# The last two attention heads in two halves of the queries, with the first group's output projection, norms, router and scatter between their tiles

## The chip, the cores and the metric

The kernel runs on one core of one Trainium2 chip. The metric is the device time of one launch in microseconds (us). The engines are named as in the profile: PE (TensorE, matmuls), PEld (its weight loads), DVE (VectorE), ACT (ScalarE), POOL (GpSimd), SP (SyncE, which here issues DMAs). ACT and POOL issue DMAs too.

## What is computed

One transformer layer in fp32, on 2048 tokens of 256 features. The attention has 16 heads of 128, unmasked, its four weight matrices as 4-bit codes with a scale per 32 rows. The second part is a mixture of 8 experts (hidden size 176), of which each token uses its best two.

```python
x = x + layernorm(attention(layernorm(x)))
x = x + layernorm(experts(layernorm(x)))
# attention
q, k, v = x @ wq + bq, x @ wk + bk, x @ wv + bv          # 2048 x (16 heads x 128)
out = softmax(q @ k.T / sqrt(128)) @ v                    # per head, 2048 x 2048 scores
return out @ wo + bo                                      # 2048 x 2048 times 2048 x 256
# experts
w, idx = top_k(softmax(x @ Wr), 2); w = w / sum(w)
h = silu(x @ Wg[e]) * (x @ Wu[e]);  y[e] = h @ Wd[e]
return sum over the token's two experts of w * y[e]
```

## The kernel before

**Order.** There is no planner: each engine runs its instructions in the order in which the code emits them, and waits by semaphore for its operands. So the place of a call in the code is its place in the queue of every engine it uses. Many tiles (`ph`, `pl`, `kT`, `v`, `oi`, `xr`, `xT0`, `xq`, `yg`, raw weights) come from one ring of 21 buffers with the tag `x` (`NX = 21`).

**The loop.** `for g in range(NS + 2)` (L851, `NS` = 256) takes one tile of 128 queries of one head per turn; head = g // 16, tile t = g % 16. The two extra turns drain the pipeline. A turn issues

- the scores of the tile against the 2048 keys in two halves (`scores_half`: 8 matmuls L525, L526, L529, and DVE's row max L530 each), the negated row max on DVE (`negmax`, L534), and two exponentials with row sums on ACT (`softmax`, L541);
- for the tile before: the reciprocal of the sums (L548, L551), the fp16 high part of the probabilities on ACT (`high_part`, L555) and, in two halves, the low part on DVE (`low_half`, L570). Each part goes through a DMA transpose issued by SP (L558, L576) into `pth` and `ptl`, which hold four tiles, a block, and come from one pool `pt` of two buffers each;
- two units of `pv_unit` (6 matmuls each, L597), which multiply the transposed probabilities of a finished block with V, 13 units behind (`PVLAG`); a block has 8. Its result is split into fp16 parts and written to `ot_d` in DRAM, but for head 15, which stays on chip (`o_last`);
- `fill(h, t)`: a part of the projections of Q, K or V of the next heads on PE (`proj_qk`, L240; `proj_v`), copied by ACT and split by POOL.

In heads 14 and 15 the loop has more: `early(t)` in head 14 makes the output bias row `crow` and issues the first loads of `oi` (attention output of four heads, read back from `ot_d`, L709); `late(t)` in head 15 loads more of them and the gate/up weights of the first half (`load_gu`, L690), splits those into two parts (`split_gu`, L681 on ACT and L683 on POOL), and runs part of the output projection.

**The output projection** `op_mm(b, half, js)` multiplies for one block b of 512 tokens (four blocks; half = 256 tokens) the head groups j in js: 16 matmuls per j (L748). With the last of j = 0 to 2 ACT moves the sum out (L764) and POOL adds `crow` (L765); with j = 3 DVE adds the rest into `at` (L759) and takes statistics (L773, L775).

**After the loop** (L902 on). For each block: first layer norm and residual (`ln_a`: a power on POOL, L81; `ln_b1`: scaling L779 and add L791 on DVE; `ln_b2`: statistics and a power; `ln_c`: scaling), transposes of the normalised rows on PE, copied by ACT and split by DVE (`tr`, L963 to L965), fp16 row pairs `xr` (`rows`, L947 on ACT, L948 on DVE), router logits and best two (`route`, 24 matmuls L976, then DVE). Blocks 0 and 1 make group 0, blocks 2 and 3 group 1. For each group `place(g)` gives every pair of token and expert a row, sorted by expert and padded to 128 rows, `scatter(b)` writes the rows to `xs_d` in DRAM with eight indirect DMAs per block (POOL, L1053), and `load_xt` reads them back transposed (SP, L1074). Then come 12 units of two 128-row tiles per group, one step each: `widen` (DVE, L1088), `gate_up` (12 matmuls L1101), `turn` (4 transposes L1120), `down` (12 matmuls L1136, ACT copy to `ysb`, L1142, DMA to `ys_d`, L1143). `gather(b)` fetches the two result rows per token (POOL, L1159), and `mix`, `scale_y` and `finish` weigh, normalise and add them (DVE L1176, ACT L1194) and write the output. The table `HOOK` says after which step other work is issued: `tr`, `route` and norms of blocks 2 and 3 at steps 1 to 7, `place(1)` and their scatter at 8, the gathers, mixes and finishes of blocks 0 and 1 from step 16 on, those of blocks 2 and 3 after the last. The tiles of the units (`xw`, `sg`, `h`, `ht`, `ysb`) come from the pool `tl` with two or three buffers each.

In before, block 0's first layer norm starts at the loop's last turn, blocks 0 and 1 are routed after the loop, and `place(0)` with the first scatter follows them and the projection of block 2.

Of the kernel before, what the change touches and what calls it, by code (L numbers as in the profile page):

```python
# [11 lines left out]
HP = mybir.dt.float16  # L12
# [26 lines left out]
def sandwich(  # L39
# [164 lines left out]
    soft_ctx, pt_ctx = ExitStack(), ExitStack()  # L204
# [20 lines left out]
    def kq_tile(which, h, b):  # L225
        if which == "q":
            return kqv.tile([128, 2, 512], HP, name="qT", bufs=3)
        if b % 2 == 0:
            KP[h] = kqv.tile([128, 2, 2, 512], HP, name="kT", tag="x", bufs=NX)
        return KP[h][:, b % 2]  # L230
# [282 lines left out]
    pt = pt_ctx.enter_context(tc.tile_pool(name="pt", bufs=2, reuse_waits="tile"))  # L513
# [3 lines left out]
    PT, PTL = {}, {}  # L517

# [34 lines left out]
    def high_part(h, t, m, p):  # L553
        ph = kqv.tile([128, S], HP, name="ph", tag="x", bufs=NX)
        nc.scalar.activation(ph, p, AF.Copy, scale=m[:, 6:7])  # L555
        if t % 4 == 0:
            PT[(h, t // 4)] = pt.tile([128, 4, 16, 128], HP, name="pth")
        nc.sync.dma_start_transpose(  # L558
            out=PT[(h, t // 4)][:, t % 4], in_=ph
        )  # L560
        return ph
# [3 lines left out]
    def low_half(half, h, t, m, p, ph):  # L565
# [7 lines left out]
        if half == 1:  # L573
            if t % 4 == 0:
                PTL[(h, t // 4)] = pt.tile([128, 4, 16, 128], HP, name="ptl")
            nc.sync.dma_start_transpose(  # L576
                out=PTL[(h, t // 4)][:, t % 4], in_=LOW.pop((h, t))
            )
# [10 lines left out]
    def pv_part(h, b, e):  # L589
# [11 lines left out]
        if e == 7:  # L601
# [5 lines left out]
            if (h, b) == (NH - 1, 3):  # L607
# [21 lines left out]
    LASTQ = {0: 1, 1: 2, 4: 3}  # L629

    def fill(h, t):
        p = h // 2
        if h == 0 and t < 5:
            proj_v(0, 6 + 2 * t, 2, "pv", wide=soft)
        if h == NH - 1:
            if t in LASTQ:
                proj_qk("q", h, LASTQ[t], wide=soft)
        elif t in QK:
            kind, dh, b = QK[t]
            if h + dh < NH:  # L640
                proj_qk(kind, h + dh, b, wide=soft)
# [8 lines left out]
    def pv_unit(u):  # L650
        n, e = divmod(u - PVLAG, 8)
        if 0 <= n < 4 * NH:
            pv_part(n // 4, n % 4, e)
# [63 lines left out]
    NS = NH * NT  # L717
# [13 lines left out]
    def op_mm(b, half, js, tag="pj", part=3):  # L731
        if js[0] == 0:
            if half == 0:
                AT[b] = kqv.tile([128, 4, D], F32, name="at", tag="x", bufs=NX)
# [63 lines left out]
    def ln_c(b):  # L798
# [4 lines left out]
    GW_LOAD = {0: 0, 2: 1, 6: 2, 8: 3}  # L803
    GW_SPLIT = {5: 0, 7: 1, 9: 2, 11: 3}
    EARLY = {8: (0, 0, 0), 10: (0, 0, 1), 12: (0, 0, 2), 14: (0, 1, 0)}
    OI_LOAD = {
        1: (0, 1, 1), 3: (0, 1, 2), 9: (1, 0, 0), 10: (0, 0, 3), 11: (1, 0, 1), 12: (0, 1, 3),
        13: (1, 0, 2), 14: (1, 0, 3),
    }
    OI_USE = {  # L810
        2: (0, (0,)), 3: (0, (1, 2)), 5: (1, (0,)), 6: (1, (1,)), 7: (1, (2,)),
        13: (0, (3,)), 14: (1, (3,)),
    }

    def early(t):
# [11 lines left out]
        if t in EARLY:  # L827
            load_oi(*EARLY[t], eng=nc.scalar)

    def late(t):  # L830
        if t == 5:
            proj_ctx.close()
            rp = ctx.enter_context(tc.tile_pool(name="gw", bufs=1, side="right"))
            guw[0] = rp.tile([128, 2, E, 2 * I], F32R, name="gu0")
        if t in OI_USE:
            op_mm(0, *OI_USE[t], "pj", 2)
        if t in GW_SPLIT:
            split_gu(guw[0], GW_SPLIT[t], gst.pop(GW_SPLIT[t]), True)
        if t in GW_LOAD:
            i = GW_LOAD[t]  # L840
            gst[i] = load_gu(0, i, nc.scalar)
        if t in OI_LOAD:
            load_oi(*OI_LOAD[t], eng=nc.scalar)
        if t == 7:
            X1[0] = kqv.tile([128, 4, D], F32, name="x1_0", tag="x", bufs=NX)
            nc.scalar.dma_start(out=X1[0], in_=XV[:, 0])


    defer = False
    prev2 = None  # L850
    for g in range(NS + 2):  # L851
        h, t = divmod(g, NT)
        live = g < NS
        if live:
            m = small.tile([128, 8], F32, name="m", bufs=6)
            s0 = scores_half(h, t, 0, m)
            if g == 0:
                proj_v(0, 0, 2)
                proj_v(0, 2, 2, "pv")
                proj_v(0, 4, 2, "s", wide=soft)  # L860
        if prev is not None:
            recip(prev[2])
        if prev2 is not None:
            low_half(1, *prev2)
        flush()
        if defer:
            pv_unit(2 * g - 1)
            defer = False
        pv_unit(2 * g)
        if prev is not None:  # L870
            prev = (*prev, high_part(*prev))
        if live:
            s1 = scores_half(h, t, 1, m)
            negmax(m)
            p = softmax((s0, s1), m)
        if prev is not None:
            low_half(0, *prev)
        prev2 = prev
        first = live and (2 * g + 1 - PVLAG) % 8 == 0
        if not first:  # L880
            pv_unit(2 * g + 1)
        if live:
            fill(h, t)
        if first and h == NH - 1:
            defer = True
        elif first:
            pv_unit(2 * g + 1)
        if live:
            prev = (h, t, m, p)
        else:  # L890
            prev = None
        if live:
            weight_steps(h, t)
        if h == 0 and t in (8, 9, 10):
            tail_consts(t - 8)
        if 7 <= g < 15:
            dequant_wo(g - 7)
        if h == NH - 2:
            early(t)
        if h == NH - 1:  # L900
            late(t)
        if g == NS - 1:  # L902
            ln_a(0)
            for j in range(4):
                load_oi(1, 1, j, eng=nc.scalar)
            op_mm(1, 0, (0, 1, 2))
        if g == NS:
            ln_b1(0)
            op_mm(1, 0, (3,))
        if g == NS + 1:  # L910
            ln_b2(0)
            ln_c(0)
            op_mm(1, 1, (0, 1, 2))
            for j in range(4):
                load_oi(2, 0, j)
    UEND = 2 * (NS + 2)

    pv_unit(UEND)
    op_mm(1, 1, (3,))
    soft_ctx.close()  # L920
    grp = ctx.enter_context(tc.tile_pool(name="grp", bufs=1, side="right", reuse_waits="tile"))
    sel_m, hot, gap, cmb, pos, eid = [], [], [], [], [], []

    before_e = grp.tile([128, E, E], F32)
    starts = grp.tile([1, NTL], F32)

    def open_groups(pool):
        nc.gpsimd.iota(starts, [[128, NTL]], base=0, channel_multiplier=0,
                       allow_small_or_imprecise_dtypes=True)
        nc.vector.tensor_tensor(  # L930
            before_e, iota8.unsqueeze(1).to_broadcast([128, E, E]),
            iota8.unsqueeze(2).to_broadcast([128, E, E]), ALU.is_lt,
        )
        for g in range(2):
            sel_m.append(pool.tile([128, GT + 1, E], BF, name=f"sel_m{g}"))
            hot.append(pool.tile([128, 2, GT, E], BF, name=f"hot{g}"))
            gap.append(pool.tile([128, GT], F32, name=f"gap{g}"))
            cmb.append(pool.tile([128, 2, GT], F32, name=f"cmb{g}"))
            pos.append(pool.tile([128, 2, GT], U32, name=f"pos{g}"))
            eid.append(pool.tile([1, NTL], I32, name=f"eid{g}"))  # L940
# [4 lines left out]
    def rows(b, on_pool):  # L945
# [57 lines left out]
    def place(g, tag="pj"):  # L1003
        ps = aux_psum([128, GT + 1, E], F32, "rk", tag)
        nc.tensor.matmul(ps, before_m, sel_m[g], start=True, stop=False)
        for t in range(GT):
# [11 lines left out]
            lower, before_e, pad.unsqueeze(1).to_broadcast([128, E, E]), ALU.mult  # L1018
# [19 lines left out]
            starts.unsqueeze(2).to_broadcast([1, NTL, E]), ALU.is_le,  # L1038
# [45 lines left out]
    def widen(g, u):  # L1084
        n = len(tiles_of(u))
        xr = tl.tile([128, 4, 256], F32R, name="xw", bufs=3)
# [6 lines left out]
    def gate_up(g, u):  # L1093
# [12 lines left out]
        sg = tl.tile([128, 2, I], F32, name="sg", bufs=2)  # L1106
        h = tl.tile([128, 2, I], F32, name="h", bufs=2)
# [6 lines left out]
    def turn(g, u):  # L1114
# [6 lines left out]
        ht = tl.tile([IH, 2, 2, 2, 128], F32R, name="ht", bufs=2)  # L1121
# [6 lines left out]
    def down(g, u):  # L1128
# [12 lines left out]
        y = tl.tile([128, 2, D], F32, name="ysb", bufs=3)  # L1141
# [39 lines left out]
    def scale_y(b, half):  # L1181
        hs = slice(2 * half, 2 * half + 2)
        R3[(b, half)] = rstd_of(MV3[b][:, hs], 2, small)
        nb = small.tile([128, 2], F32, name="nb", bufs=2)
# [35 lines left out]

    nc.scalar.activation(sgv, ssc[:, 0:1], AF.Sigmoid)
    open_groups(grp)
    uwp = ctx.enter_context(tc.tile_pool(name="uw", bufs=1, side="right", reuse_waits="tile"))
    guw[1] = uwp.tile([128, 2, E, 2 * I], F32R, name="gu1")
    ln_a(1)
    load_x1(1)
    loads(2, 1)
    tr(0, 0, "s")
    tr(0, 1, "s")
    rows(0, True)  # L1230
    ust = [load_gu(1, i) for i in range(2)]
    ln_b1(1)
    for e in range(1, 3):
        pv_unit(UEND + e)
    op_mm(2, 0, (0, 1, 2), "s")
    ln_b2(1)
    route(0)
    for e in range(3, 5):
        pv_unit(UEND + e)
    op_mm(2, 0, (3,), "s")  # L1240
    ln_c(1)
    split_gu(guw[1], 0, ust[0], True)
    split_gu(guw[1], 1, ust[1], True)
    ust = [load_gu(1, i) for i in range(2, 4)]
    for e in range(5, 9):
        pv_unit(UEND + e)
    tr(1, 0, "s")
    tr(1, 1, "s")
    rows(1, True)
    route(1)  # L1250
    pt_ctx.close()
    tl = ctx.enter_context(tc.tile_pool(name="tl", bufs=1, reuse_waits="tile"))
    dw = tl.tile([IH, 2, E, 2, D], F32R)
    op_mm(2, 1, (0, 1, 2, 3), "s")
    place(0)
    scatter(0)
    scatter(1)
    load_x1(2)
    ln_a(2)
    loads(3, 0)  # L1260
    split_gu(guw[1], 2, ust[0], False)
    split_gu(guw[1], 3, ust[1], False)
# [97 lines left out]
```

## Time and profile before

| | us |
|---|---|
| three runs | 1834.75, 1836.46, 1836.72 (median 1836.46) |
| the profiled execution | 1836.82 |
| its span, first to last instruction | 1835.0 |
| loop, to the negated row max of the last tile (L534) | 1543.3 |
| from there to the end of the span | 291.7 |
| first matmul of the experts (L1101) | 1644.1 |
| first of the second group | 1721.7 |

The mean granted TensorE clock is 0.963 of full speed. The profile is of one execution. Rows of a timeline have the start, the length, engine, line and operation with its tiles, and in brackets the idle time before it and what ended it. Busy sums of DMA queues are shares of 16 engines; a stretch may show a share over 1, as packets of several queues overlap on an engine.

### The profile page before, as it was taken

How to read it: one execution, taken by the hardware profiler on the slowest of the kernel's cores; microseconds unless marked ns; L12 is line 12 of the kernel's file. 1: busy time of each engine (PE TensorE's matmuls, PEld its weight loads, DVE VectorE, ACT ScalarE, POOL GpSimd, SP SyncE). 2: the span in 40 equal slices, each digit the busy share in tenths (PEclk: the TensorE clock that was granted, in tenths of full speed). 3: DMA queues.
4: the chain of work that ended last, by engine and by line, in shares of the span. 5: the costliest groups of instructions: out<-in, count | busy, mean ns of one | idle time of the engine just before them, and what ended most of it. 6: DMA issues, size and time to landing. Idle time of an engine off the chain costs nothing. (4 is left out here: it accounts for less than half of the span.)

```text
span 1835.0 us, 25558 instructions
## 1 busy us (share of the span) xinstructions
PE 1700.0 (93%) x8536; PEld 881.6 (48%) x8536; DVE 1598.3 (87%) x2250; ACT 1363.2 (74%) x1747; POOL 978.1 (53%) x976
## 2 busy tenths in 40 slices
PE   7899999999999999999999999999999998949660
PEld 4344444444444444444444444444444454749660
DVE  6999999999999999999999999999999887557252
ACT  5888888888888888888888888888888875213141
POOL 5596566556655665556565656565454331161423
PEclk9899999999999999999999999999999999878785
DMA  9999999999999999999999999999999999861622
GB/s 292 186 195 207 196 202 198 206 198 201 200 197 202 199 199 195 207 197 193 206 200 198 197 202 206 195 202 201 191 189 205 222 226 228 237 180 51 157 95 80
DMA packets 1128477, 355.08 MB, mean 194 GB/s; under 512 B 1095244, under 2 KB 1112092, under 8 KB 1128348
## 3 DMA queue, kind: packets, MB, share of 16 engines
q1 hardware_dynamic: 1104300, 302.20, 90.1%
q0 software_dynamic: 12672, 35.17, 6.7%
q10 hardware_dynamic: 11376, 16.09, 2.8%
q8 instruction: 69, 1.13, 0.2%
q14 instruction: 60, 0.49, 0.1%
HBM read 44.83 MB, written 34.08 MB: 43 GB/s over the span
## 5 line engine op out<-in xcount | busy, mean ns | idle before, releaser
L541 ACT ACTIVATE p<-s,m,ssc 128x1024 f32<-128x1024 f32 x512 | 612.3, 1200 | 183.1 <-DVE m L534 169.4
L570 DVE SCALAR_TENSOR_TENSOR pl<-p,m,ph 128x1024 f16<-128x1024 f32 x512 | 733.1, 1432 | 6.6 <-ACT ph L555 5.9
L530 DVE TENSOR_REDUCE m<-s 128x1 f32<-128x1024 f32 x512 | 621.8, 1214 | 19.4 <-PE s L529 18.5
L555 ACT ACTIVATE ph<-p,m 128x2048 f16<-128x2048 f32 x256 | 513.0, 2004 | 55.2 <-ACT t L253 15.0
L597 PE MATMUL pv<-pth,v 128*128 128x512 f16 x2048 | 504.2, 379 | 1.1 <-DMA pth<-ph 0.9
L597 PEld LDWEIGHTS <-v 128*128 128x128 f16 x3072 | 300.5, 98 | 363.9 <-issue 4.1
L525 PE MATMUL s<-kT,qT 128*128 128x512 f16 x1024 | 388.9, 380 | 10.9 <-ACT p L541 10.0
L526 PE MATMUL s<-kT,qT 128*128 128x512 f16 x1024 | 389.0, 380 | 0.7 <-POOL kT L255 0.7
L529 PE MATMUL s<-kT,qT 128*128 128x512 f16 x1024 | 305.5, 380 | 0.0
L597 PE MATMUL pv<-ptl,v 128*128 128x512 f16 x1024 | 251.9, 379 | 0.0
L285 POOL CAST v<-t 128x256 f16<-128x256 f32 (+1 forms) x118 | 51.0, 432 | 279.3 <-ACT t L284 279.3
L254 POOL CAST qT<-t 128x512 f16<-128x512 f32 x63 | 77.8, 1235 | 222.8 <-ACT t L253 222.8
L286 POOL TENSOR_TENSOR v<-t,v 128x256 f16<-128x256 f32 (+1 forms) x118 | 177.3, 1502 | 9.6
L529 PEld LDWEIGHTS <-qT 128*128 128x128 f16 x1024 | 100.4, 98 | 122.3 <-issue 2.1
L526 PEld LDWEIGHTS <-qT 128*128 128x128 f16 x1024 | 100.2, 98 | 122.2 <-issue 17.6
L525 PEld LDWEIGHTS <-qT 128*128 128x128 f16 x1024 | 100.2, 98 | 108.5 <-issue 1.1
L541 ACT ACTIVATION_READ_ACCUMULATOR p<-s,m,ssc 128x1 f32 x512 | 99.1, 194 | 0.0
L617 POOL TENSOR_TENSOR o<-t,o 128x512 f16<-128x512 f32 x60 | 96.2, 1603 | 4.9
L255 POOL TENSOR_TENSOR kT<-t,kT 128x512 f16<-128x512 f32 x61 | 93.5, 1532 | 5.2
L1101 PE MATMUL s<-gu,xw 128*128 x276 | 58.0, 366 | 33.4 <-DVE xw L1088 31.6
L255 POOL TENSOR_TENSOR qT<-t,qT 128x512 f16<-128x512 f32 x63 | 85.6, 1359 | 5.1
L548 DVE TENSOR_SCALAR m<-m 128x1 f32<-128x1 f32 x256 | 53.9, 211 | 36.0 <-ACT p L541 24.5
(198 smaller groups left out, 1610.4 us busy)
## 6 DMA issues: line engine op xcount, KB each, us to landing
ot_d<-o POOLq DMA_DIRECT2D x60, 256.0 KB
oi<-ot_d ACTq DMA_DIRECT2D x12, 512.0 KB
oi<-ot_d SPq DMA_DIRECT2D x12, 512.0 KB
ys_d<-ysb ACTq DMA_DIRECT2D x22, 256.0 KB
xs_d<-zero SPq DMA_DIRECT2D x10, 512.0 KB
pth<-ph SPq DMA_TRANSPOSE x256
ptl<-pl SPq DMA_TRANSPOSE x256
xt<-in_L_attn_x SPq DMA_DIRECT2D x4, 512.0 KB
```

Source lines behind the costliest of these rows:

```text
L254: nc.gpsimd.tensor_copy(t[:, 0, :], t32)
L255: nc.gpsimd.tensor_tensor(t[:, 1, :], t32, t[:, 0, :], ALU.subtract)
L286: nc.gpsimd.tensor_tensor(v[:, 1, sl, :], t32, v[:, 0, sl, :], ALU.subtract)
L525: nc.tensor.matmul(s[:, j, :], q[:, 0, qc], k[:, 0, :], start=True, stop=False)
L526: nc.tensor.matmul(s[:, j, :], q[:, 0, qc], k[:, 1, :], start=False, stop=False)
L529: nc.tensor.matmul(s[:, j, :], q[:, 1, qc], k[:, 0, :], start=False, stop=True)
L530: nc.vector.tensor_reduce(m[:, half : half + 1], s, AX.XY, ALU.max)
L541: nc.scalar.activation(p[:, bass.ts(i, 1024)], s, AF.Exp, bias=m[:, 2:3], scale=ssc[:, 0:1], accum_out=m[:, 3 + i : 4 + i],)
L555: nc.scalar.activation(ph, p, AF.Copy, scale=m[:, 6:7])
L570: nc.vector.scalar_tensor_tensor(pl[:, cs], p[:, cs], m[:, 6:7], ph[:, cs], ALU.mult, ALU.subtract)
L597: nc.tensor.matmul(ps, V[(h // 2, c // 4)][:, i % 2, c % 4, dc], d[:, :, c, :], start=(n == 0), stop=(n == 47),)
L617: nc.gpsimd.tensor_tensor(o[:, :, 1, :], halves(t32), o[:, :, 0, :], ALU.subtract)
```

## The change

The loop's order changes in the last two heads (32 tiles, from turn `LATE` = 224). Write r = g - 224. Tiles 0 to 7 of head 14 run at r = 0 to 7, tiles 0 to 7 of head 15 at 8 to 15, then tiles 8 to 15 of head 14 at 16 to 23, and of head 15 at 24 to 31. With that the first half of all tokens (blocks 0 and 1) has all its heads finished half-way, and its further work is issued between the tiles of the second half:

- K and Q of head 15 and the rest of Q are projected at r = 0 to 9, one each (`LATE_QK`); head 13 projects the last V pair two token tiles at a time, and one Q part. The bias row moves from head 14 to head 12.
- `op_mm` of blocks 0 and 1 runs at r = 10 to 17 (j = 0 to 2: two j's on even r, one on odd) and 20, 21, 24, 25 (j = 3). Each `oi` is loaded by ACT one tile ahead (`OI_PLAN`).
- `CHAIN` puts the norms of blocks 0 and 1 at r = 22 to 28, `tr`, `rows` and `route` at r = 26 to 31.
- the two turns after the last tile issue `place(0)`, `op_mm` of block 2 (j = 0 to 2) and the first scatter.
- The gate/up weights of the first half are loaded and split after the loop, each second piece on POOL, the others on DVE; so are those of the second half and `dw` (from `draw`), whose loads now stand behind the transposed loads.
- In `HOOK`, `place(1)` and its scatter go from step 8 to step 6; both gathers of group 0 stand at step 16, its mixes at 21 and 22, its `scale_y` at 23 and 24, and its `finish` after the gathers of blocks 2 and 3.
- `pt` becomes two pools of one buffer each; `at` and the residual rows of blocks 0 to 2 get a pool `ex`; the units' `xw`, `ht`, `ysb` and a joint tile for `sg` and `h` come from the ring `x`.

```diff
+    NS = NH * NT
+    LATE = NS - 2 * NT
+    def place_of(g):
+        if g < LATE:
+            return divmod(g, NT)
+        half, r = divmod(g - LATE, NT)
+        return NH - 2 + r // 8, 8 * half + r % 8
...
+    LATE_QK = {
+        0: ("k", 15, 0), 1: ("k", 15, 1), 2: ("k", 15, 2), 3: ("k", 15, 3), 4: ("q", 15, 0),
+        5: ("q", 15, 1), 6: ("q", 14, 2), 7: ("q", 14, 3), 8: ("q", 15, 2), 9: ("q", 15, 3),
+    }
-    def fill(h, t):
+    def fill(g, h, t):
         p = h // 2
+        if g >= LATE:
+            if g - LATE in LATE_QK:
+                proj_qk(*LATE_QK[g - LATE], wide=soft)
+            return
...
+        elif h == NH - 3:
+            if t < 12:
+                proj_v(p + 1, 4 + t - 1, 2, wide=soft)
+            elif t == 13:
+                proj_qk("q", NH - 2, 1, wide=soft)
...
+    OP_PLAN = {
+        10: (0, 0, (0, 1)), 11: (0, 0, (2,)), 12: (0, 1, (0, 1)), 13: (0, 1, (2,)),
+        14: (1, 0, (0, 1)), 15: (1, 0, (2,)), 16: (1, 1, (0, 1)), 17: (1, 1, (2,)),
+        20: (0, 0, (3,)), 21: (0, 1, (3,)), 24: (1, 0, (3,)), 25: (1, 1, (3,)),
+    }
+    OI_PLAN = {}
+    for r, (b, half, js) in OP_PLAN.items():
+        for j in js:
+            OI_PLAN.setdefault(r - 1, []).append((b, half, j))
...
+    def late(r):
...
+        if r in OP_PLAN:
+            op_mm(*OP_PLAN[r], "pj", 2)
+        for i in OI_PLAN.get(r, ()):
+            load_oi(*i, eng=nc.scalar)
...
+        for f in CHAIN.get(r, ()):
+            f()
...
+    CHAIN = {
+        22: [lambda: ln_a(0), lambda: ln_b1(0)],
+        23: [lambda: ln_b2(0)],
+        24: [lambda: ln_c(0)],
+        26: [lambda: tr(0, 0), lambda: ln_a(1), lambda: ln_b1(1)],
+        27: [lambda: tr(0, 1), lambda: rows(0), lambda: ln_b2(1)],
+        28: [lambda: route(0), lambda: ln_c(1)],
+        29: [lambda: tr(1, 0)],
+        30: [lambda: tr(1, 1), lambda: rows(1)],
+        31: [lambda: route(1)],
+    }
...
-        h, t = divmod(g, NT)
         live = g < NS
+        h, t = place_of(g) if live else (NH, g - NS)
...
+        if g >= LATE:
+            late(g - LATE)
+        if g == NS - 2:
+            for j in range(3):
+                load_oi(2, 0, j, eng=nc.scalar)
+            X1[2] = ex.tile([128, 4, D], F32, name="x1_2")
+            nc.scalar.dma_start(out=X1[2], in_=XV[:, 2])
+        if g == NS - 1:
+            for j in range(3):
+                load_oi(2, 1, j, eng=nc.scalar)
+        if g == NS + 1:
+            for j in range(3):
+                load_oi(3, 0, j)
+            for half in range(2):
+                load_oi(2, half, 3)
+        if g == NS:
+            place(0)
+            op_mm(2, 0, (0, 1, 2), "pj", 2)
+        if g == NS + 1:
+            op_mm(2, 1, (0, 1, 2), "s", 2)
+            scatter(0)
+            scatter(1)
...
+    op_mm(3, 0, (0, 1, 2), "pj", 2)
...
+    op_mm(3, 1, (0, 1, 2), "s", 2)
+    for i in range(4):
+        split_gu(guw[0], i, gst.pop((0, i)), i % 2 == 1)
+    op_mm(2, 0, (3,), "pj", 2)
+    op_mm(2, 1, (3,), "s", 2)
+    ln_a(2)
...
+    for i in range(4):
+        gst[(1, i)] = load_gu(1, i)
...
+    ln_b1(2)
...
+    for i in range(4):
+        split_gu(guw[1], i, gst.pop((1, i)), i % 2 == 1)
+    ln_b2(2)
...
+    experts(0)
+    for q in range(6):
+        load_xt(0, q)
+    op_mm(3, 0, (3,), "pj", 2)
+    op_mm(3, 1, (3,), "s", 2)
+    ln_a(3)
+    ln_c(2)
+    draw = [load_d(q) for q in range(4)]
+    for q in range(2):
+        split_d(q, draw[q])
...
     HOOK = {
-        1: [lambda: tr(2, 0), lambda: ln_b1(3)],
...
-        8: [lambda: place(1), lambda: scatter(2), lambda: scatter(3)],
+        0: [lambda: tr(2, 0), lambda: tr(2, 1), lambda: rows(2)],
+        1: [lambda: ln_b1(3), lambda: split_d(2, draw[2]), lambda: split_d(3, draw[3])],
+        2: [lambda: ln_b2(3), lambda: route(2)],
+        3: [lambda: ln_c(3)],
+        4: [lambda: tr(3, 0), lambda: tr(3, 1), lambda: rows(3)],
+        5: [lambda: route(3)],
+        6: [lambda: place(1), lambda: scatter(2), lambda: scatter(3)],
...
+        NU + 4: [lambda: gather(0, range(4)), lambda: gather(1, range(4))],
+        NU + 9: [lambda: mix(0, range(4))],
+        NU + 10: [lambda: mix(1, range(4))],
+        NU + 11: [lambda: scale_y(0, 0), lambda: scale_y(0, 1)],
+        NU + 12: [lambda: scale_y(1, 0), lambda: scale_y(1, 1)],
```

## The prediction

> **What bounds the kernel now.** The first view is the page: busy time per engine and the 40 slices of 45.9 us.
>
> ```profile
> PE 1700.0 (93%) x8536; PEld 881.6 (48%) x8536; DVE 1598.3 (87%) x2250; ACT 1363.2 (74%) x1747; POOL 978.1 (53%) x976
> PE   7899999999999999999999999999999998949660
> DVE  6999999999999999999999999999999887557252
> PEclk9899999999999999999999999999999999878785
> ```
>
> The loop over 16 heads fills PE; the last seven slices do not. So there are two stages, and the change moves work from the second, slack one into the first, full one. The second view is the busy time by stretch (columns: stretch, length, then PE, PEld, DVE, ACT, POOL busy with counts, PE clock, DMA share, GB/s).
>
> ```profile
> 1200.00:1400.00 200.00, 199.50 (x956) 93.40 (x955) 192.33 (x239) 169.22 (x213) 106.01 (x104) 1.00 1.07 194
> 1620.00:1644.00 24.00, 0.00 (x0) 0.00 (x0) 12.48 (x26) 0.00 (x0) 16.25 (x15) 0.59 0.67 157
> 1691.00:1722.00 31.00, 13.00 (x84) 12.15 (x83) 7.09 (x15) 5.20 (x10) 15.54 (x16) 0.74 0.48 128
> 1740.00:1757.00 17.00, 5.42 (x35) 4.51 (x33) 1.74 (x3) 1.29 (x3) 10.70 (x12) 0.71 0.38 111
> 1792.00:1835.00 43.00, 0.00 (x0) 0.00 (x0) 10.96 (x36) 7.93 (x17) 18.10 (x20) 0.53 0.25 80
> ```
>
> In the loop PE has 0.5 us in 200 free, and DVE only 8: work put there is paid nearly in full. In the tail PE stands still for 24 us (first scatter), 18 of 31 (second scatter), 12 of 17, and the last 43. The chain of waits says what ends those gaps (start, us, what).
>
> ```profile
> 1544.37 14.37 DMA ptl<-pl
> ...
> 1609.73 1.11 POOL xs_d L1053
> ...
> 1629.27 0.96 POOL xs_d L1053
> ...
> 1644.11 3.87 PE s L1101 x12
> ...
> 1711.83 2.27 DMA xs_d<-xr,pos
> 1714.28 6.69 DMA xq<-xs_d
> ...
> 1740.01 7.49 another core or an unknown queue
> ```
>
> Sixteen row scatters take 1609.7 to 1630.2 (20.3 us with their gaps), their landing 2.3, the transposed load 6.7, and the experts' first matmul comes at 1644.1. The last line is a stall of the experts: ACT cannot write the next `ysb` (three buffers) while the rows of `ys_d` leave slowly beside the gathers.
>
> The third view, DVE's timeline, gives what a tile costs; the time between two L534 rows (the negated row max, one per tile) is a tile.
>
> ```profile
> 1516.29 0.27 DVE L534 TENSOR_SCALAR m<-m,ssc 128x1 f32<-128x1 f32 x1
> 1521.94 0.27 DVE L534 TENSOR_SCALAR m<-m,ssc 128x1 f32<-128x1 f32 x1
> 1527.59 0.27 DVE L534 TENSOR_SCALAR m<-m,ssc 128x1 f32<-128x1 f32 x1
> 1528.97 0.75 DVE L759 SCALAR_TENSOR_TENSOR at<-op,sig,at 128x512 f32<-128x512 f32 x1
> 1534.50 0.27 DVE L534 TENSOR_SCALAR m<-m,ssc 128x1 f32<-128x1 f32 x1
> ```
>
> A tile with nothing beside it is 5.65 us (DVE sets it), one with an output evict and its statistics 6.9. In head 15 a tile with 16 projection matmuls went 1456.40 to 1463.57 (7.17), one with 32 to 1472.29 (8.72), and there DVE waited on PE.
>
> **The sum.** I split the execution at L534 of tile 224 (the first that the change reorders, 1350.7), and of tile 255 (1543.26): 192.6 us of loop, then 291.7 to the end of the 1835.0 span. The execution's own time is 1836.82, 1.8 more than its span and 0.4 above the median 1836.46.
>
> *Head 13* gets 12 V tile projections in place of 8 (0.43 us of PE each) and one Q projection (0.855): +2.6, since PE is full there.
>
> *r = 0 to 9* (tiles 224 to 233): each carries one K or Q projection, 4 matmuls, 0.855 us. The other 24 matmuls of 512 columns take 5.12, so PE sets 6.0: 60.0. The new order of heads by itself moves no work; each block still has its 8 PV units, and two one-buffer pools alternate as one of two buffers did.
>
> *r = 10 to 17*: four tiles with 32 and four with 16 projection matmuls: 4 x (8.72 + 7.17) = 63.6, by the rows above.
>
> *Loads of `oi`* for these tiles are now issued one tile ahead; before, two to four. The issue stands on ACT behind both exponentials, 3.5 us after L534 (1467.11 against 1463.57), the matmuls 0.2 us ahead of the next L534 (1472.08 against 1472.29). So the lead is the tile less 3.7: 2.3 us at r = 10, 3.4 at 12, 14, 16, 5.0 at 11, 13, 15, 17. No row shows how long a load takes in the loop. From below: 512 KB in that queue's packets (11376 packets, 16.09 MB, 2.8% of 16 engines: 1414 bytes, 72 ns), each alternating with a transpose packet of 24 ns, is 23 x 96 ns = 2.2 us, and the undisturbed `ys_d` write landed 1.7 after its issue: an estimate of 3.9 for one load and 6.1 for the second of a pair, which leaves waits of 2.0 + 3 x 1.0 = 5 us. From above: the `draw` loads issued at 1597.8 were used at 1605.2, 7.4 us: 5.1 + 3 x 4.0 + 4 x 2.4 = 27. I take 10, nearer to the first, whose packets are those of this loop; range 5 to 27.
>
> The Trainium skill, "DMA: Bandwidth & Descriptors", rules for kernel authors, says to issue a DMA early and wait for it late, which speaks against a lead of one tile. Its fit for one DMA (issued from GpSimd, not ACT: about 2.0 us and bytes / 436e3) makes 3.2 us of 512 KB, an estimate from that page, and by it alone these waits would be about 1 and the time some 9 us lower.
>
> *r = 18, 19*: 11.3. *r = 20 to 25*: four tiles with an evict (6.9 each, ACT's and DVE's share), and with the first group's ln_a/ln_b1 (four scalings 1.38, add 1.23, statistics 1.40 + 0.36) and ln_c (1.37) on DVE: 6.9 + 6.9 + 9.45 + 7.35 + 8.3 + 6.9 = 45.8.
>
> *r = 26 to 31*: transposes `tr`, router rows and routing. PE gets 4 x 0.44 + 2 x 2.6 = 7.0 more, which alone would fit under a DVE-set loop. But DVE's part of `tr` (0.68) needs ACT's copy of the same PSUM tile, and ACT issues that behind the tile's exponentials (2.9 us after L534), so DVE stands about 2.4 more per `tr`; rows cost 1.2 of DVE, a route 1.85. Sum 12.05 + 11.5 + 8.65 + 8.05 + 9.65 + 7.3 = 57.2.
>
> Together, less the last tile, which ends behind its L534: 60 + 63.6 + 10 + 11.3 + 45.8 + 57.2 - 7.3 = 240.6, with head 13 243.2, against 192.6: **the loop loses 50 us**. If the round trips of DVE hide (PE's and DVE's own sums are each about 207), it loses 15 to 30.
>
> *After the loop*, from L534 of tile 255. The 14.4 us transpose wait of `ptl` and the `at` buffer's 7.0 us PE wait go; `place(0)` and the output projection (2,0), (2,1) (48 matmuls, 5.3 each) with four PV units (1.3 each) put the scatter at about 21; its queue, POOL, has the evicts' adds ahead of it, and behind it the adds of (3,*), half of `gu0`'s and `gu1`'s splits (1.7 to 2.4 each) and the power steps of ln(2), ln(3) (1.0). Scatter ends at 41, landing and transposed load would allow experts at 55 as they followed 13.9 us after it before; DVE's widening stands behind ln_c(2), which waits for POOL: 61, where it was 100.9. SP's queue gets the `gu1` loads ahead of the transposed loads, both waiting for the scatter's landing, and the `draw` loads behind them, so the first `down` waits for `dw` splits to about 77. Twelve units at 1.95 + 0.44 + 1.44 = 3.83 with tr and route of blocks 2, 3: `place(1)`, now at step 6 and not 8, at 99; 20.3 of scatter, 2.3, 6.7: second group at 129 (178.4 before). Its units take 51; the `ysb` tiles now come from a ring of 21 buffers and gathers and mixes stand later, so the 12 us stall goes, at 6 us of mix and scale beside units and 0 to 8 for slow rows: 59 (70.1 before). The last 43 stay: gathers, mix and finish of blocks 2, 3; finish(0), (1) go under the gathers' wait. 129 + 59 + 43 = 231 against 291.7: **the tail gains 61**, 45 to 70 by its bounds.
>
> Net 50 - 61 = -11 of span: 1836.5 - 10.5 = **1826 us**.
>
> **Rivals.** *The late tiles hide.* If ACT and DVE run ahead enough that the round trips of r = 20 to 31 and the loads cost half, 22 us come off: 1804. For it: ACT is idle 15% of the steady stretch. Against it: DVE is 96% busy there, and in the evict tile above it waits on ACT already.
>
> *The wait returns.* Experts need `gu0`, `gu1`, `dw` splits, which stood under the loop and the first scatter and now stand behind it on POOL and SP. If the first `down` comes 10 us later than I have it, 1836: no measurable change, which here is 0.2%, 3.7 us. For it: POOL's queue behind the scatter; against it: DVE takes half of the pieces at 0.85 each.
>
> *Late loads, slower.* The `oi` loads land one tile ahead too late. Place: PE in front of its projection matmuls at r = 10 to 17, and at 20 and 21. With 7.4 us to landing the eight tiles cost 27 (not 10): 1843; the four loads of r = 20 to 25 add up to 13, together 1856; I take 1848. It decides from 6.6 us to landing, where the waits are 20 and the whole gain is gone. For it: the DMA share is over 1.0 throughout the loop, and a transpose there took 14.4 us beside 1.9 MB of such loads. Against it: those were four loads within 5 us.
>
> **How the numbers follow.** Forecast 0.38 (1826, own range 1817 to 1834, faster); hidden 0.17 (1804, faster); wait returns 0.15 (1836: 0.10 the same, 0.05 slower); late loads 0.30 (1848, slower). Faster 0.55, same 0.10, slower 0.35. Leaving out some 0.08 below and 0.12 above, the range is 1802 to 1850.
>
> **What would show it.** Right: tiles 224 to 233 at 6.0 us, 234 to 241 in pairs of near 16, 250 to 255 at 8 to 12; the scatter 21 and the experts 61 us behind L534 of tile 255; no `ysb` wait beside the gathers; 43 us at the end. Wrong: PE idle in front of L748's matmuls with `oi` named as releaser for more than 20 us in all; experts later than 75; or tiles 250 to 255 below 8.

## The result, and the profile after

The changed kernel took 1883.04 us (median of 1875.76 to 1883.77), the kernel before 1835.61 beside it: 1.0259 of before, 95% interval 1.022 to 1.0298. The profiled execution of the changed kernel took 1883.77, its span is 1882.0. The forecast was 1826, 57 us less.

The page of the changed kernel, busy time and the 40 slices (47 us each now):

```profile
PE 1719.4 (91%) x8536; PEld 886.2 (47%) x8536; DVE 1596.4 (85%) x2253; ACT 1368.0 (73%) x1747; POOL 974.8 (52%) x966
PE   7899999999999999999999999999997987868760
DVE  6999999999999999999999999889995698457343
PEclk9999999999999999999999999999998998878885
```

The tail's dip is shorter, but DVE is down to 8 in the 26th and 27th slice, long before the reordered tiles, and to 5 and 6 in the 31st and 32nd, in the middle of them. Tile by tile (L554 is the negated row max here, L534 before), the difference splits like this:

| stage | forecast | measured |
|---|---|---|
| up to tile 224, more than before | 2.6 | 14.1 |
| r = 0 to 9 | 60.0 | 60.3 |
| r = 10 to 17, with the loads' waits | 73.6 | 80.2 |
| r = 18 to 25 | 57.1 | 57.2 |
| r = 26 to 30 | 49.9 | 48.4 |
| last tile's L554 to the first scatter | 21 | 26.5 |
| its start to the experts' first matmul | 40 | 51.3 |
| from there to the second group's first matmul | 68 | 80.4 |
| the second group's units, to their last matmul | 59 | 68.9 |
| the rest | 43 | 44.0 |

So the loop lost 53.5 us between tiles 224 and 255 (245.9 against 192.4) and 14 before that, and the tail gained 20.6 (271.1 against 291.7), not 61. Where the second group begins is read from PE's timeline: each group ends with a unit of 6 matmuls, the only one that is not of 12.

```profile
1766.20 1.13 PE L1056 MATMUL s<-gu,xw 128*128 x6
...
1769.04 2.09 PE L1056 MATMUL s<-gu,xw 128*128 x12
```

The timeline of the changed kernel in head 12, tile 9, shows what the 14 us are:

```profile
1217.28 0.36 ACT L288 COPY t<-pj 128x256 f32<-128x256 f32 x1
1217.70 2.59 PE L695 MATMUL pb<-wo,bv 128*3 128x256 bf16 x16 [3.29 <-ACT t L288]
1222.67 1.22 DVE L550 TENSOR_REDUCE m<-s 128x1 f32<-128x1024 f32 x1 [6.67 <-PE s L549]
```

The bias row's matmuls write the PSUM buffer (tag `pj`, one buffer) that the tile's V projection has just used. They wait 3.3 us for ACT's copy, which stands behind the exponentials, and everything behind them on PE waits too; DVE then stands 6.7. The same happens at tile 11. At tiles 9 and 11 of head 14, where the row was made before, there is no V projection.

The waits of PE from tile 224 to 255 (engine, line and releaser; us in total, times, longest):

```profile
PE op L775 <- DMA oi<-ot_d: 15.0, 8, 7.9
```

And the places of the tail, in the order of time, from the timelines of PE, POOL, ACT and DVE:

```profile
1619.02 8.28 PE L775 MATMUL op<-wo,oi 128*128 128x256 bf16 x48 [4.49 <-DVE rank L978]
...
1637.37 1.10 POOL L1008 DMA_INDIRECT xs_d<-xr,pos  x1 [0.17 <-issue]
...
1648.22 0.27 PE L775 MATMUL op_s<-wo,oi 128*128 128x256 bf16 x1 [0.24 <-issue]
1649.62 0.39 PE L775 MATMUL op_s<-wo,oi 128*128 128x256 bf16 x2 [1.14 <-issue]
...
1662.70 3.68 DVE L711 TENSOR_TENSOR gu<-gu_raw,gu 128x704 fp32r<-128x704 f32 x2 [24.87 <-ACT gu L709]
...
1685.14 1.35 PE L918 MATMUL trp<-ident,at 128*128 128x128 f32 x4 [5.96 <-DVE at L806]
...
1688.67 3.87 PE L1056 MATMUL s<-gu,xw 128*128 x12
...
1694.13 5.50 DVE L806 TENSOR_SCALAR at<-at,mv,ln_r 128x256 f32<-128x256 f32 x4
...
1755.40 0.59 ACT L1097 COPY ysb<-dps 128x512 f32<-128x512 f32 x1 [7.25 <-remote]
...
1792.61 0.46 ACT L1064 ACTIVATE sh<-s 128x352 f32<-128x352 f32 x1 [8.01 <-remote]
1798.26 0.58 ACT L1077 CAST ht<-s 88x512 fp32r<-88x512 f32 x1 [5.19 <-remote]
1801.84 0.59 ACT L1097 COPY ysb<-dps 128x512 f32<-128x512 f32 x1 [3.00 <-remote]
```

Read from the top: block 2's projection waits 4.5 us for DVE to read the result of `place(0)`, again out of the `pj` buffer, and then takes 8.28 us at a mean granted clock of 0.64, where the next 48 matmuls take 5.40 at 1.00. In the first scatter PE issues 16 matmuls one or two at a time (1648 to 1661), with no wait that the profile shows. DVE's first piece of `gu` waits for ACT's cast; the experts' first matmul stands behind the transposes of block 2, and those behind block 2's norm on DVE. A scaling of four instructions that takes 1.37 us elsewhere takes 5.5. At the end of the second scatter ACT stands 7.25 us and in the gathers 16.2 us with a releaser that the profile does not name (`remote`), as it did before; the ring of buffers has not taken that away.

### The profile page after: what moved, and what is told of

It is laid out like the page before. It is cut to its first block, busy times and chain, and to the rows that moved or that the text cites. A ratio compares the mean times of both kernels' runs of the same rounds, so it can differ in the third digit from the quotient of the medians.

```text
span 1882.0 us, 25550 instructions
## 1 busy us (share of the span) xinstructions
PE 1719.4 (91%) x8536; PEld 886.2 (47%) x8536; DVE 1596.4 (85%) x2253; ACT 1368.0 (73%) x1747; POOL 974.8 (52%) x966
## 5 line engine op out<-in xcount | busy, mean ns | idle before, releaser
L545 PE MATMUL s<-kT,qT 128*128 128x512 f16 x1024 | 391.0, 382 | 24.2 <-ACT p L561 24.2
L290 POOL TENSOR_TENSOR v<-t,v 128x256 f16<-128x256 f32 (+1 forms) x112 | 167.5, 1495 | 9.1
L258 POOL CAST kT<-t 128x512 f16<-128x512 f32 x61 | 63.6, 1042 | 46.7 <-ACT t L257 45.4
L257 ACT ACTIVATE t<-pj,bqs 128x512 f32<-128x512 f32 x123 | 83.9, 682 | 0.0
```

What stands on the lines that cost most here:

```text
L258: nc.gpsimd.tensor_copy(t[:, 0, :], t32)
L290: nc.gpsimd.tensor_tensor(v[:, 1, sl, :], t32, v[:, 0, sl, :], ALU.subtract)
L545: nc.tensor.matmul(s[:, j, :], q[:, 0, qc], k[:, 0, :], start=True, stop=False)
```

## The experiments

**The bias row.** The row's two sums come from the scores' ring of three PSUM buffers:

```diff
-        pb = psA.tile([128, 512], F32, name="pb", tag="pj")
+        pb = s_pair()[:, 0]
```

> The changed kernel with the two sums of the bias row taken from the scores' PSUM ring (three buffers) and not from the one buffer that the projections use. Theory 1: head 12 costs 12.9 us more than before because PE waits there twice for ACT's copy of the V projection out of that one buffer, and only 2.6 us are the row's 16 matmuls. Then head 12 comes within 3 us of before, and the run is 9 to 11 us faster than the changed kernel (1872 to 1875). Theory 2: the row itself, or its place beside the V projections, costs the time: less than 4 us faster.

Measured: 1872.25 us, 1.0224 of before (1.0181 to 1.0267); head 12 takes 96.7 us, where the changed kernel has 106.9 and before 92.2; theory 1 asked for under 3 above before, and it is 4.5. In the profile the 16 matmuls wait for nothing:

```profile
1214.59 1.91 PE L695 MATMUL s<-wo,bv 128*3 128x256 bf16 x16
```

The other way round, in the kernel before only the head of the row is changed (`h == NH - 2` to `h == NH - 4`, its `oi` loads staying in head 14):

> The kernel before with nothing changed but the bias row, made in head 12 and not in head 14. Theory 1: it meets the V projections of head 12 in the one PSUM buffer and costs 12 to 14 us by itself (1848 to 1850). Theory 2: the cost in the changed kernel comes from elsewhere (the other projections or buffers): under 3 us.

Measured: 1845.8 us, 1.0072 (1.004 to 1.0104); head 12 takes 106.5 instead of 92.2. So the move alone costs 14 us in this profile, 10 by the run's median (a little under theory 1's 12 to 14). The larger part goes with the shared buffer: head 12 takes 101.7 to 106.9 us in the eight profiles that make the row there in this buffer, and 96.3 to 96.7 in the four that use the scores' ring.

**The loads of `oi`.** Three tiles ahead (`OI_PLAN.setdefault(r - 3, [])`):

> The changed kernel with every load of oi issued three tiles ahead instead of one. Theory 1: tiles r = 10 to 17 take 80 us, not 63.6, because PE waits for the loads (15.0 us in the changed profile, 7.9 of it for the second load of r = 10, which landed 13 us after its issue). Then these eight tiles come to 64 to 68 and the run is 11 to 16 us faster (1868 to 1873). Theory 2: the DMA engines are full, so the same bytes only delay the transposes instead: under 5 us faster.

Measured: 1863.84 us, 1.0169 (1.0124 to 1.0214); the eight tiles take 68.8 us instead of 80.2, and PE waits for no load there. All profiles bear it out: 67.6 to 69.8 us in the four with the loads three tiles ahead, 75.5 to 87.2 in the seven with one. Both theories hold a part: tile r = 10 still takes 13.1 us, because now DVE waits for the transposes of `pl`, 12.7 us in three places, which it does not do in the changed kernel. That the loads hold the transposes up on the shared DMA engines fits the DMA share (1.16 from 1420 to 1434 us) but was not tested by itself. The longest of the three:

```profile
1432.45 1.28 DVE L590 SCALAR_TENSOR_TENSOR pl<-p,m,ph 128x1024 f16<-128x1024 f32 x1 [7.71 <-DMA ptl<-pl]
```

**Who holds ACT in the gathers?** The second group's writes of `ys_d` go to SP's queue:

```diff
-        nc.scalar.dma_start(
+        (nc.scalar if g == 0 else nc.sync).dma_start(
             out=ys_d[g][256 * u : 256 * u + 128 * n].rearrange("(c p) d -> p c d", p=128),
```

> The changed kernel with the second group's writes of ys_d issued by SP and not by ACT. In the gathers' 20 us ACT stands still three times, 16.2 us in all, each time for a releaser that the profile does not name. Theory 1: ACT is held by its own write DMAs while POOL's row gathers run; then the 16 us shrink to under 4 and the run is 10 to 15 us faster. Theory 2: ACT is held by something that the gathers do to any waiting engine, or by buffers whose writes have not landed: under 4 us either way.

Measured: 1880.83 us, 1.0279 (1.0211 to 1.0348). ACT still stands 6.6, 6.6 and 3.0 us at the same three instructions. It is not held by its own writes.

The trace says more than the views do. The three instructions read what PE writes: the sigmoid reads the result of `gate_up`, the cast that of `turn`, the copy that of `down`. In the kernel before it is the same, and the first one held is the sigmoid, not the copy to `ysb`:

```profile
1747.53 0.46 ACT L1109 ACTIVATE sg<-s 128x352 f32<-128x352 f32 x1 [7.97 <-remote]
```

The semaphore that ends the wait is the one that PE's matmuls raise. This holds for all 45 nameless waits of ACT of over 2.5 us behind the loop, in the ten profiles that have them: ACT starts 0.02 us after PE's semaphore goes up. In the changed kernel it goes up at 1792.58, 1798.23 and 1801.82, while the records put the matmuls in question at 1783.3 to 1787.3:

```profile
1783.30 2.10 PE L1056 MATMUL s<-gu,xw 128*128 x12
1785.24 0.60 PE L1075 MATMUL s<-ident,sh 128*88 128x128 f32 x4
1785.59 1.67 PE L1091 MATMUL dps<-dw,ht 88*128 x12
```

No instruction is recorded as ending at those times, so the view names none. ACT thus waits for PE, whose signal comes 7 to 15 us behind the recorded end of its matmuls.

**Four edits, two in the tail.** The two above, `place(0, "s")`, and the gathers of blocks 0 and 1 spread:

```diff
-        NU + 4: [lambda: gather(0, range(4)), lambda: gather(1, range(4))],
-        NU + 9: [lambda: mix(0, range(4))],
...
+        NU + 4: [lambda: gather(0, [0])],
+        NU + 5: [lambda: gather(0, [1])],
...
+        NU + 9: [lambda: gather(1, [1]), lambda: mix(0, range(4))],
...
+        NU + 13: [lambda: mix(1, range(4))],
```

> The changed kernel with four edits at four places, each read from its own stage: bias row in the scores' PSUM ring; oi loads three tiles ahead; place(0) in the scores' ring too, since the projection of block 2 waited 4.5 us for DVE to read its result out of the shared buffer and then ran at half clock; and the gathers of blocks 0 and 1 two per step instead of sixteen in a row. Theory: the first two add up (28 us by their own runs), the third brings the scatter 5 to 7 us nearer to the last tile (from 26.5), and the spread takes ACT's 16 us of standing still beside the gathers down to under 5: 1835 to 1842. Rival for the gathers: each holds ACT up wherever it stands; then the stall is only spread out and the run is 1846 to 1852.

Beside it, the changed kernel with only its PV units moved, and the kernel before with only the spread (its mixes, scalings and finishes placed as in the four edits):

```diff
-    for e in range(1, 3):
+    for e in range(1, 9):
         pv_unit(UEND + e)
     op_mm(3, 1, (0, 1, 2), "s", 2)
...
-    for e in range(3, 6):
-        pv_unit(UEND + e)
     ln_b1(2)
-    for e in range(6, 9):
-        pv_unit(UEND + e)
```

> The changed kernel with the last six PV units moved ahead of the output projection (3,1). In the changed profile that projection's last 16 matmuls come one at a time from 1648 to 1661, in the middle of the first scatter, with no wait that the profile shows. Theory 1: PE is held up by the scatter, whatever it runs; then the PV units or the projection still lose about 12 us in the scatter's second half, and the run is within 5 us of the changed kernel (1878 to 1888). Theory 2: it is the projection's own loads of oi, just issued; then PV fills the time, the projection runs at full speed behind it, the experts start 8 to 12 us earlier and the run is 1871 to 1875.

> The kernel before with the gathers of blocks 0 and 1 two per step instead of eight at once, their mixes and scalings later and their finishes behind the last gathers. Theory: the 16 us for which ACT stood still beside the gathers (1740 to 1757) shrink to under 5, and the tail's second group is 8 to 14 us shorter: 1822 to 1828. Rival: the gathers hold ACT up wherever they stand: within 4 us of before.

Measured, all three beside a before of 1823.89: four edits 1834.3 (1.0059, 1.0039 to 1.008), PV units first 1858.93 (1.0194, 1.0175 to 1.0213), before with the spread 1813.87 (0.9936, 0.9912 to 0.996). `place(0)` is settled: with another buffer the projection follows at once, at a granted clock of 1.00, and the scatter starts 18.9 us behind the last tile instead of 26.5:

```profile
1592.40 0.19 PE L960 MATMUL rk_s<-sel_m,before_m 128*128 128x72 bf16 x1 [1.26 <-DVE sel_m L952]
1592.43 0.35 PE L963 MATMUL rk_s<-sel_m,all_m 128*128 128x64 bf16 x8
1592.64 5.40 PE L775 MATMUL op<-wo,oi 128*128 128x256 bf16 x48
```

The gathers could not be judged in that session (a session here is a set of kernels measured side by side on one chip): none of its profiles has an unnamed wait of ACT, not even the one where only PV units moved, and there the second group's units took 55.7 us with sixteen gathers in a row. So the kernel before with the spread became faster there without a wait to take away; what gave it the 10 us is not shown, as no profile of the unchanged kernel before was taken in such a session. The order was measured once more beside the unchanged kernels:

> The changed kernel itself once more, so that the kernels of this call can be compared with it on one chip. The run with the PV units ahead had none of ACT's nameless waits (20 us and more in the changed profile), nor had any kernel measured beside it, also where neither the scatter nor the gathers were touched. Theory 1: these waits and PE's single matmuls belong to the chip or session and not to the kernel: where they are absent, the changed kernel itself takes 1856 to 1864 beside a before of about 1824. Theory 2: they belong to the changed order: they are there again, and it takes 1875 to 1884.

> The kernel before once more, for its profile beside the changed one's on the same chip. Theory 1 (the waits belong to the chip or session): ACT's 7.9, 4.5 and 3.7 us beside the gathers and 12 us beside the second scatter are absent where the changed kernel's are absent, and the span is near 1823. Theory 2: they are there, 1835.

> The PV units ahead of the projection (3,1) once more, now beside the changed kernel. Theory 1 (waits belong to the chip or session): within 4 us of the changed kernel measured with it. Theory 2 (the order takes them away): 10 to 20 us faster than it.

> The changed kernel with the spread gathers alone. Theory 1: if ACT's waits beside the gathers are absent on this chip anyway, the spread gives what the later mixes and scalings give, 0 to 6 us. Theory 2: the spread itself frees the units: 10 to 16 us faster than the changed kernel measured with it.

Measured beside a before of 1832.02: the changed kernel 1887.77 (1.0292, 1.0244 to 1.0341), the profiled before with a span of 1833.4, PV units first 1883.12 (1.0277, 1.0241 to 1.0313), the spread alone 1878.52 (1.0274, 1.0218 to 1.033). The waits are back in before (7.3, 5.9 and 3.7 us in the gathers, 12.2 in the second scatter), in the changed kernel and in the one with the PV units first, which had none of them in the other session. They belong to the chip or the session, then, not to the order: the profiles of three sessions show them in either order of the loop, those of the other three in none. On this chip, which has them, the spread takes ACT's waits in the gathers away (not those in the scatters); the second group's units are 62.1 us instead of 68.8, and the run is 9 us faster, though its four times spread over 25. The waits and PE's single matmuls in the first scatter come in the same three sessions, and in both it is PE that is late while POOL issues indirect DMAs in a row. What delays PE there stays open.

**Experts behind the first scatter.** Four edits, the PV units first, and the `draw` loads ahead of the transposed loads:

> The four edits together, and two more: the PV units ahead of the projection (3,1), and the draw loads on SP ahead of the transposed loads of the first group. In the run with four edits ACT waits 14.3 us for draw, and its casts of dw stand ahead of the copies of tr(2) that the first expert matmul waits for (71.8 us behind the last tile). Theory: with draw early the experts start 60 to 66 us behind the last tile, the tail comes to 232 to 238 and the run is level with before or up to 0.4% faster; the loop keeps its 42 us loss. Rival: the draw bytes only push the transposed loads back: the experts at 70 or later, ratio to before still 1.004 or more.

Measured: 1831.9 us beside 1824.92, 1.0039 (1.0017 to 1.0061). The experts start 68.9 us behind the last tile, not at 60 to 66 and not at 70 either; the ratio is the rival's. ACT's waits for `draw` are 3.6 us instead of 14.3, but DVE is now the last: it starts on the pieces of `gu` at 1636.0, behind ACT's casts, and is busy for 21.0 of the 22.5 us to the end of its first widening, with 4.1 us for a scaling that takes 1.4 elsewhere, beside POOL's split.

**POOL against DVE.** The low parts of `dw` on DVE (`split_piece(..., False)`):

> The kernel with six edits, but the low parts of dw are computed by DVE and not by POOL. In all runs of the changed order the scaling of block 3 (four instructions, 1.37 us elsewhere) takes 5.5 us on DVE beside POOL's splits of dw. Theory 1: the two engines hold each other up; then the scaling is back at 1.4 to 1.7 us, and although DVE gets four pieces of about 1 us, the first group's second and third unit come 2 to 5 us earlier: 2 to 4 us faster than the kernel with six edits. Theory 2: the scaling waits for something else: it stays at 5 us or more, and DVE's 4 us more make the run slower by 1 to 4.

Measured: 1835.27 us, 1.0058 (1.0039 to 1.0078). The timelines of DVE, with POOL's splits and then without them beside it:

```profile
1665.84 5.50 DVE L806 TENSOR_SCALAR at<-at,mv,ln_r 128x256 f32<-128x256 f32 x4
```

```profile
1669.22 1.38 DVE L806 TENSOR_SCALAR at<-at,mv,ln_r 128x256 f32<-128x256 f32 x4
```

The effect of theory 1 is there, four times the length; its gain is not, since the pieces now lie on DVE itself and the experts start at 74.8 instead of 68.9. The Trainium skill, "SBUF — State Buffer", Terms, says that DVE and GpSimd share one port pair under an exclusive lock. The pair of rows agrees with it; no run here isolates the lock.

**The parts that need no new loop.** The kernel before with the spread gathers (above) and with the second scatter at step 6:

```diff
-        8: [lambda: place(1), lambda: scatter(2), lambda: scatter(3)],
...
+        3: [lambda: route(2), lambda: ln_c(3)],
+        4: [lambda: tr(3, 0), lambda: tr(3, 1), lambda: rows(3, False)],
+        5: [lambda: route(3)],
+        6: [lambda: place(1), lambda: scatter(2), lambda: scatter(3)],
```

> The kernel before with the spread gathers, and with one more part of the change done alone: place(1) and the second scatter at step 6 instead of 8, with tr and route of blocks 2 and 3 closed up. Theory: the second scatter starts 6 to 8 us earlier in the units, while the units left behind it cover more of its 30 us: 4 to 8 us faster than with the spread alone, 0.989 to 0.992 of before. Rival: the router's round trips crowd the first units and push them back by as much: within 2 us of the spread alone.

> The kernel before with spread gathers and the second scatter at step 6, once more. Theory: what these two parts of the change give does not need the loop's new order, on any chip: 0.988 to 0.995 of before again, more where ACT's waits beside the gathers are there to be taken away. Rival: the gain belonged to the session: within 0.2% of before.

> The kernel before with the spread gathers alone, beside the one with the second scatter at step 6. If step 6 pays by itself, this run is 4 to 10 us slower than it, and 0.992 to 0.997 of before; if it does not, they are within 3 us.

Measured: 1811.94 us beside 1824.92 (0.9934, 0.9909 to 0.996), and again 1814.0 beside 1825.32 (0.9942, 0.9919 to 0.9965), with the spread alone at 1817.56 (0.995, 0.9933 to 0.9966). Both beat both kernels. Step 6 on top of the spread is worth some 4 us in that session, between its theory and its rival and at the edge of what can be told; in the profiles the second group's first matmul comes 167.0 us behind the last tile instead of 172.8. In the first profile with step 6 PE's wait for the transposed rows, 24.2 us for the first group, is 9.8 for the second:

```profile
1708.93 3.89 PE L1101 MATMUL s<-gu,xw 128*128 x12 [9.75 <-DVE xw L1088]
```

## Why the prediction was wrong, step by step

Three steps failed. The bias row's move stood in the sum at nothing, and cost some 12 us. The chain from the last tile to the experts was added up without the wait for a shared PSUM buffer and without DVE's queue, 17 us too short. And the stall beside the gathers was read as a lack of `ysb` buffers and taken out of the sum; it is ACT's wait for a late PE, it returned (10 us), and a second one in the second scatter came to count (7 us). The parts in order of time:

- **The loop's loss, right in mechanism.** Forecast 50, of it 48 from tile 224 on; measured 53.5. The plain tiles, the evict tiles and the round trips of `tr`, `rows` and `route` came within 2 us of each sum. That the late tiles hide, the first rival, is refuted: they did not.
- **The loads, mis-sized within their bounds.** Taken 10 us, bounds 5 to 27, measured 15.0. The estimate of 3.9 and 6.1 us to landing failed for the second load of r = 10: 13.3 us from its issue (1420.9) to its matmul (1434.2). The third rival, priced at 1848 for the loads, named the place but not the size.
- **The bias row, missing.** The sum has the V and Q projections of head 13 and nothing for the bias row's move to head 12. Head 12 took 14.7 us more than before, head 13 0.9 where 2.6 were summed. 10 of the 14.7 went when the row got another buffer, and the move alone brought 14 to the kernel before: what failed is that the moved row was not followed to what it meets in its new place.
- **The scatter's start, 5.5 too early.** The sum had PE's and POOL's durations and no wait between `place` and the projection behind it; they share the same one buffer. With another buffer it is 18.9 to 20.6, better than the forecast 21.
- **From the scatter to the experts, 11 too short.** Forecast 20 from the scatter's end (13.9 as before and six more), measured 31.2, and 28 to 36 in every version of the changed order. The sum let DVE wait for POOL; the rows show DVE's own queue. It starts 5.2 us behind the scatter's end, then takes 23.9 us to the end of its first widening, of which it is busy 20.1 (pieces of `gu`, evicts, statistics and norms of blocks 2 and 3), and the transposes of block 2 take the last 2.1. Two pieces of `gu` there take 3.7 us beside POOL's splits and 1.7 where POOL is idle (1649.7 in the run with six edits), the 0.85 each of the sum. This is the second rival, the wait that returns, but its reason was POOL's queue and its price 10 us on the first `down`: that came at 95.1 instead of 77.
- **The second group's start, 12 too late.** Behind the experts' first matmul `place(1)` and the second scatter came 6 us later than summed, for reasons not looked into. The other 7 are ACT's wait at the end of the second scatter (7.25 us in the rows above): it holds the first group's last units, and the second group stands behind them. In the kernel before the same wait is 12.1 us, but lies under the wait for the transposed rows and costs nothing there.
- **The second group's units, 10 too long.** The ring was to remove ACT's stall of 16 us. It did not, since ACT waits for PE and not for a buffer. Where a session has no such waits the units take 53 to 56 us, below the 59 of the sum; where it has them, with sixteen gathers in a row, 68 to 72 in both kernels. That the sum comes near in the other sessions is luck: it took the stall away for a cause that was not the one.

Together 11.5 + 5.3 + 5.5 + 11.3 + 12.4 + 9.9 + 1.0 is the 57 us between forecast and result. Of the signs named ahead, the pairs of tiles (15.7 to 17.7 us, but for the first, 30), tiles 250 to 255 and the 43 us at the end came nearly as in the forecast; the experts at 77.8 are beyond the 75 that was to show it wrong.

With six edits the changed order is 1.0039 of before. Measured beside each other, its tail is 239.3 us and that of the kernel before with spread and step 6 is 267.3: the order itself gives 28. Its loop costs 39 from tile 224 on and 5 in heads 12 and 13; another 5 of the difference between the two profiles lies ahead of head 12, where the two kernels do the same. That is where the expected gain went: a loop in which PE and DVE are both full takes nothing in for free, and 11 to 13 us were to be had inside the tail alone.

## What to carry to other kernels

Before a step is moved, list the buffers that it writes as well as its engines: a PSUM tag with one buffer makes a queue of its own, and its price is the wait for the engine that empties it, with all that stands ahead in that engine's queue (3.3 and 4.5 us here). When work leaves an idle stage for a full one, price it at its full length, and look first for an order within the idle stage. Where a stage ends on several engines that wait for each other, sum along the chain and not per engine. Where a view names no releaser, ask what the waiting instruction reads, and when that engine's semaphore went up, before a cause is put into the sum.

## What the hardware showed

- While POOL issued indirect DMAs in a row (one per 1.25 to 1.27 us), ACT stood still up to 12 us at a time in three of six sessions (16.7 once), in both kernels, whichever queue carried the writes, and each of the 45 waits of over 2.5 us ended with PE's semaphore; with two per step it did not beside the gathers. In the changed kernel PE there issued 16 matmuls in 13 us without a wait for any semaphore. Why PE is late in these sessions is not known.
- Four DVE scalings took 5.50 us beside POOL's splits and 1.38 without them.
- The matmul that needed a 512 KB load came 13.3 us behind its issue, in a stretch of the loop with a DMA share of 1.24. With the loads issued earlier DVE waited for transposes instead, 7.7 us at one tile.
